# Relational graph layer: node products in chunks of four groups with the weights stationary, a ring of eight slots and 46 message buffers

## The chip, the cores and the metric

One core of a Trainium2 chip runs the kernel. Its engines are TensorE (PE; its weight loads are listed as PEld), VectorE (DVE), ScalarE (ACT), GpSimd (POOL) and SyncE (SP). The metric is the device time of one launch in microseconds, the median of several runs.

## The reference

12,500 nodes with 256 features, 212,500 edges sorted by destination (100,000 random ones in both directions and one loop edge per node), each with one of eight types. `weight` has 8 x 256 x 256, `loop_weight` 256 x 256 values; all is float32.

```python
def reference(x, src, dst, edge_type_8, weight, h_bias, loop_weight):
    h = relu((x - mean(x)) / sqrt(var(x) + 1e-05))          # per row
    hx = einsum('ni,rio->rno', h, weight)
    msg = hx[edge_type, src]
    agg = segment_sum(msg, dst, num_segments=12500)
    return x + agg * 0.5 ** 0.5 + h_bias + (h @ loop_weight) * 0.5 ** 0.5
```

## The kernel before

The kernel exchanges the two steps: it first sums, for every node and type, the h rows of the node's incoming edges, and then multiplies these sums by the weights. Edges are worked in tiles of up to 128 (1583 of them); two tiles are a unit (792 units, each of at most 271 edges' advance). Four stages run side by side, and their instructions are issued in an order that Python writes out by hand in one loop over the tiles t.

- **Gather** (`gather`, L779 to L793). POOL issues one indirect DMA for a tile: 128 rows of 1 KB of h (or of x, for the first tiles, normalized afterwards on DVE and ACT in batches of four) go to a message buffer. `MSGS` = 66 buffers stand in pairs; at tile t the gather of tile t + `AHEAD` (64) is issued, so POOL waits when PE has not yet finished the sums of the pair whose buffers it needs. A gather is a DMA of the software queue.
- **Sums** (`edge_sums`, L822). For both halves of the features PE multiplies the message rows (stationary) by a one-hot matrix (moving, L795) of 22 or 13 nodes x 8 types, that is 176 or 104 columns. A float32 product runs as two passes, each with its own weight load, so a tile has four loads and four matmuls on L837. The sums of a unit stay in one of four PSUM banks until DVE adds them to the ring (`add_sums`, L847, L851) one unit later.
- **The ring** `acc` (L288) holds, transposed, the sums of the nodes at hand: 128 features x 2 halves x 8 types x nodes. It has `SLOTS` = 6 slots of 128 nodes. A group is 128 nodes, one slot. `Plan` gives for each group the first unit that may touch its nodes (`first`) and the last one (`last`). A slot is prepared for group g + 6 when group g is done: by `clear` (ACT, zeros), or later by `begin` (L890), which lets PE transpose the group's own h rows to the tile `pt`, DVE write them, multiplied by the loop edge's type, in eight writes (L900), and ACT keep a copy `self_t` (L883). The types of the loop edges are found per four groups by `mark` and `find_types` (L913 to L967). When the ring comes round, `wrap` (L1007) adds its overhang.
- **Products** (`group_work`, L1014). For each group 18 products (loop weight and eight types, two halves of the inputs each) are accumulated in a PSUM tile `po`: the group's sums (128 features x 128 nodes) are stationary, the weights (256 columns) move. With two passes each that is 36 loads and 36 matmuls on L1029. Then `finish` adds a bias copy and the product to the rows of x (L1041, L1042), and after four groups stores 512 rows by one DMA on SP. `finish` also prepares the slot for group g + 6. `group_ahead` (L985) loads the next x and h rows.

When do products run? Once the last unit of group g is added, its 18 products enter `queue` with the earliest tile `ready` (six tiles on), the latest tile `until` (before the unit `first` of group g + 6) and a cost each; at every tile so many are taken that all are in time (L1233 to L1240). For the last eight groups (`SOON`) `until` is at most six tiles after `ready`. Jobs that need `pt` go one after the other through `shared` and `advance` (L677 to L703), DVE's writes of own rows are held back by `credit` (L1191, L1221), and `late` holds what falls due at a tile.

At the start, the gathers of the first 64 tiles are issued, and 26 pieces of x are normalized to the table h in DRAM, three in four tiles. When the last is through (`norms_end`, L1150), the weights are loaded and scaled, and gathers read h from 72 tiles on.

Of the kernel before, what the change touches and what calls it, by code (L numbers as in the profile page):

```python
# [43 lines left out]
SLOTS = 6  # L44
# [3 lines left out]
MSGS = 66  # L48
AHEAD = 64
# [170 lines left out]
def kernel(  # L220
# [63 lines left out]
    with ExitStack() as main:  # L284
# [12 lines left out]
        early = main.enter_context(tc.tile_pool(name="early", bufs=1))  # L297
        marks = main.enter_context(tc.tile_pool(name="marks", bufs=1))
        selves = main.enter_context(tc.tile_pool(name="selves", bufs=SLOTS + 1))
# [13 lines left out]
        outs = [ps_o.tile([P, 2, D], F32, name=f"po{i}") for i in range(2)]  # L313
# [533 lines left out]
        def add_sums(u, ps):  # L847
            a = acc[:, :, :, bass.ds(offsets.pop(u), WIN)]
            a = dataclasses.replace(a, dep_tracking_offset=order)
            ps = ps.rearrange("p c (d r) -> p c r d", r=R)  # L850
            i = nc.vector.tensor_tensor(a, a, ps, op=ALU.add)  # L851
            added[u] = i.ins
            for g in range(1, plan.NG):
                if plan.first[g] == u:
                    while plan.first[g] and (g, "slot") not in zeroed:
                        advance(None)
                    assert not plan.first[g] or (g, "slot") in zeroed
                    for k in [k for k in zeroed if k[0] == g or k[1] == "wrap"]:
                        tc.add_manual_dep(
                            i.ins, zeroed.pop(k).name, SYNC_DEP, reason="columns are empty")  # L860

# [8 lines left out]
        def turn_nodes(g, pool, written=None):  # L870
# [10 lines left out]
            def keep():  # L881
                got["self", g] = pool.tile([P, KC, GROUP], F32, name="self_t")
# [7 lines left out]
        def begin(g):  # L890
# [4 lines left out]
            turn, keep, pst = turn_nodes(g, selves, written)  # L895
# [89 lines left out]
        def group_ahead(g):  # L985

            q, k = divmod(g, XG)

            def load(q):
                load_groups("x", x, q)  # L990
                if q < plan.typed:
                    load_groups("h", h32, q)

            work = []
            if g == 0:
                work.append((0.0, lambda: load(0)))
            if q < plan.typed:
                def turned_nodes():
                    turn, keep, _ = turn_nodes(g, early)
                    shared(turn, [(1, keep)])  # L1000

                work.append((0.4, turned_nodes))
            if k == XG - 2:
                work.append((0.0, lambda: load(q + 1)))
            return work
# [8 lines left out]
        def group_work(g):  # L1014
# [3 lines left out]
            first_dep = [True]  # L1018

            def product(r, c):  # L1020
                if (r, c) == (R, 0):
                    got["out", g] = outs[g % 2][:, 0, :]
# [4 lines left out]
                else:  # L1027
                    lhs, rhs = acc[:, c, r, s0 : s0 + n], w[:, c, r * D : (r + 1) * D]
                i = nc.tensor.matmul(got["out", g][:n], lhs, rhs, start=(r == R and c == 0),  # L1029
                                     stop=(r == R - 1 and c == KC - 1))  # L1030
                latest["pe"] = i.ins
                if (r, c) == (R, 0) and g < 2:
                    tc.add_manual_dep(i.ins, done["bias"], SYNC_DEP, reason="one engine at a time")
                if r < R and first_dep[0]:
                    first_dep[0] = False
                    tc.add_manual_dep(i.ins, added[plan.last[g]].name, SYNC_DEP, reason="sums complete")

            def finish():
                q, k = divmod(g, XG)
                rows_ = got["x", q]  # L1040
                nc.vector.tensor_add(rows_[:n, k, :], rows_[:n, k, :], outs[g % 2][:n, 1, :])  # L1041
                nc.vector.tensor_add(rows_[:n, k, :], rows_[:n, k, :], got["out", g][:n])  # L1042
                if XG * (q + 1) >= plan.NG:
                    nc.sync.dma_start(out[d0 : d0 + n], rows_[:n, k, :])
                elif k == XG - 1:
                    first = plan.starts[XG * q]
                    nc.sync.dma_start(
                        out[first : d0 + n].rearrange("(k p) d -> p k d", p=P), rows_)
                b = g + SLOTS
                q, k = divmod(b, XG)  # L1050
                if b < plan.NG:
                    if q < plan.typed:
                        clear(b)
                    else:
                        begin(b)
                if q + 1 >= plan.typed and XG * (q + 1) < plan.NG:
                    if k == XG // 4:
                        load_groups("h", h32, q + 1)
                    if k == XG - 2:
                        mark(q + 1)  # L1060
                    if k == XG - 1:
                        find_types(q + 1)

            def last():
                done["late"].append((done["tile"] + REST, finish))

            work = []
# [6 lines left out]
        with tc.manual_schedule():  # L1074
# [56 lines left out]
            def load_weights():  # L1131
                bias_in = got["bias"] = rowp.tile([P, XG, D], F32, tag="rows", name="biasr")[:, 0, :]
                nc.sync.dma_start(
                    bias_in, bass.AP(tensor=bias.tensor, offset=bias.offset, ap=[[0, P], [1, D]]))
# [6 lines left out]
            def scale_weights():  # L1141
                for o in outs:
                    i = nc.vector.tensor_copy(o[:, 1, :], got["bias"])
                done["bias"] = i.ins.name
# [27 lines left out]
            next_group = 0  # L1172
# [13 lines left out]
            for t in range(NT):  # L1186
# [56 lines left out]
                while waiting and (len(waiting) > LAG or t == NT - 1):  # L1243
                    u, ps = waiting.pop(0)
                    add_sums(u, ps)
                    while (next_group < plan.NG and plan.last[next_group] <= u
                           and (done["weights"] or (NT <= 400 and done["norm"] == len(pieces)))):
                        g = next_group
                        while background and NT <= 400:
                            step()  # L1250
                        until = PAIR * (plan.first[g + SLOTS] - 3) - REST if g + SLOTS < plan.NG else NT - 1
                        ready = t + max(0, min(DELAY, NT - 1 - t - 2 * DELAY))
                        if g >= plan.NG - SOON:
                            ready = min(ready, t + 1)
                        until = max(ready, min(until, ready + int(GROUP / plan.rate * PAIR)))
                        if g >= plan.NG - SOON:
                            until = min(until, ready + DELAY)
# [45 lines left out]
```

## Time and profile before

| what | value |
|---|---|
| median of 3 runs | 2439.66 us (2438.91 to 2439.7) |
| the profiled execution | 2440.51 us, its span 2438.7 us |
| mean granted clock of TensorE | 0.893 |
| PE, PEld, DVE, ACT, POOL busy | 79%, 70%, 54%, 9%, 62% |
| gathers | 1483 from h, 100 from x, 207.59 MB in all |
| waits of POOL's gathers | issue 438.9 us (1324), unknown queue 219.5 us (122), PE sums L837 91.8 us (79) |
| waits of DVE's adds L851 | unknown 377.3 us, PE sums L837 272.6 us |
| DMA, mean | 114 GB/s |

Busy PE counts modelled ends of overlapping matmuls, so the distance from one start to the next says more than a duration. "issue" is time in which an engine waits for nothing that the profile shows. The profile's clock row gives tenths of full speed for 40 slices of the span.

### The profile page before, as it was taken

How to read it: one execution, taken by the hardware profiler on the slowest of the kernel's cores; microseconds unless marked ns; L12 is line 12 of the kernel's file. 1: busy time of each engine (PE TensorE's matmuls, PEld its weight loads, DVE VectorE, ACT ScalarE, POOL GpSimd, SP SyncE). 2: the span in 40 equal slices, each digit the busy share in tenths (PEclk: the TensorE clock that was granted, in tenths of full speed). 3: DMA queues.
4: the chain of work that ended last, by engine and by line, in shares of the span. 5: the costliest groups of instructions: out<-in, count | busy, mean ns of one | idle time of the engine just before them, and what ended most of it. 6: DMA issues, size and time to landing. Idle time of an engine off the chain costs nothing.

```text
span 2438.7 us, 28985 instructions
## 1 busy us (share of the span) xinstructions
PE 1934.7 (79%) x10339; PEld 1700.9 (70%) x10339; DVE 1326.8 (54%) x3382; ACT 222.2 (9%) x475; POOL 1508.5 (62%) x1609
## 2 busy tenths in 40 slices
PE   0257788787888888888888888888888888888889
PEld 0246677776777777777777777777777777777788
DVE  3387734546744545754445754445754445765453
ACT  3474310000000000000000000000000000000000
POOL 7535666666666666666666666666666666666640
PEclk9557989999989898998889998899899889998999
DMA  6584433343334343333343333343333343333320
GB/s 204 161 296 137 125 89 117 89 127 114 91 117 119 89 124 116 91 117 105 105 123 91 116 116 93 115 127 89 117 117 89 118 118 92 117 106 101 111 71 14
DMA packets 147869, 278.87 MB, mean 114 GB/s; under 512 B 29759, under 2 KB 97064, under 8 KB 147720
## 3 DMA queue, kind: packets, MB, share of 16 engines
q0 software_dynamic: 75984, 207.59, 29.2%
q1 hardware_dynamic: 70136, 69.38, 8.9%
q8 instruction: 82, 1.34, 0.2%
q14 instruction: 67, 0.55, 0.1%
q10 hardware_dynamic: 1600, 0.01, 0.0%
HBM read 251.26 MB, written 25.60 MB: 114 GB/s over the span
## 4 chain that ended last, share of the span: by engine, by line
PE 66%; issue 14%; DVE 11%; another core or an unknown queue 4%; ACT 2%; DMA 1%; POOL 1%; DVEq 0%; SPq 0%; ACTq 0%; POOLq 0%
PE ps L837 33%; PE po L1029 31%; DVE acc L851 2%; DVE oh L804 1%; DVE e_stats L741 1%; DVE acc L900 1%; PE pt L878 1%; DVE n_stats L741 1%; DVE moves L380 1%; DVE n_mv L743 1%; POOL msg L791 1%; DMA w<-in_L_gnn_weight_dram 1%; DVE fixed L382 0%; ACT diagonal L954 0%
## 5 line engine op out<-in xcount | busy, mean ns | idle before, releaser
L791 POOL DMA_INDIRECT msg<-h,gidx x1483 | 1411.6, 952 | 761.5 <-issue 389.6
L837 PE MATMUL ps<-oh,msg 128*128 128x176 f32 (+1 forms) x6332 | 1178.9, 314 | 303.2 <-issue 163.0
L837 PEld LDWEIGHTS ps<-oh,msg 128*128 128x128 f32 x6332 | 1090.1, 208 | 444.6 <-issue 217.5
L1029 PE MATMUL po<-w,acc 128*128 128x256 f32 x3136 | 975.0, 413 | 87.5 <-issue 75.5
L851 DVE TENSOR_TENSOR acc<-acc,ps 128x352 f32 x792 | 409.0, 516 | 764.4 <-remote 377.3
L1029 PEld LDWEIGHTS po<-w,acc 128*128 128x128 f32 x3136 | 577.8, 206 | 164.8 <-issue 132.2
L804 DVE TENSOR_TENSOR oh<-fixed,cols 128x704 f32<-128x704 f32 x397 | 348.9, 879 | 0.0
L900 DVE SCALAR_TENSOR_TENSOR acc<-types,pt 128x256 f32<-128x256 bf16 (+1 forms) x688 | 248.7, 411 | 89.2 <-PE ps L837 48.5
L883 ACT ACTIVATE self_t<-pt 128x256 f32<-128x256 f32 x98 | 37.5, 383 | 1754.2 <-DVE acc L900 1030.5
L791 POOL DMA_INDIRECT msg<-in_x_dram,gidx x100 | 95.0, 950 | 83.1 <-issue 49.3
L1029 PE MATMUL po<-wl,self_t 128*128 128x256 f32 x392 | 116.6, 410 | 14.3 <-issue 7.7
L1029 PEld LDWEIGHTS po<-wl,self_t 128*128 128x128 f32 x392 | 70.9, 201 | 35.5 <-issue 24.0
L878 PE MATMUL pt<-ident,hr 128*128 128x128 f32 x196 | 41.7, 288 | 29.0 <-issue 25.7
L1041 DVE TENSOR_TENSOR xr<-xr,po 128x256 f32<-128x256 f32 x98 | 40.6, 415 | 31.1 <-remote 14.5
L753 ACT ACTIVATE msg<-msg,e_shift,e_rstd 128x256 f32<-128x256 f32 x100 | 51.8, 589 | 21.3 <-DVE e_shift L750 12.0
L753 ACT ACTIVATE xt<-xt,n_shift,n_rstd 128x256 f32<-128x256 f32 x98 | 50.9, 589 | 18.5 <-DVE e_stats L741 6.1
L878 PEld LDWEIGHTS pt<-ident,hr 128*128 128x128 f32 x196 | 25.9, 156 | 30.2 <-issue 25.9
L954 ACT ACTIVATE diagonal<-ident,kinds 128x128 bf16<-128x128 f32 x88 | 28.1, 390 | 172.7 <-DVE kinds L950 158.6
L1042 DVE TENSOR_TENSOR xr<-xr,po 128x256 f32<-128x256 f32 x98 | 41.2, 421 | 3.4
L380 DVE TENSOR_SCALAR moves<-fixed 128x271 int32<-128x271 int32 (+1 forms) x90 | 40.5, 450 | 2.2 <-issue 0.9
L382 DVE COPY_PREDICATED fixed<-moves,fixed 128x311 int32<-128x311 int32 (+14 forms) x90 | 38.0, 422 | 3.1
L741 DVE BATCH_NORM_STATS2 e_stats<-msg 128x6 f32<-128x256 f32 x100 | 34.9, 410 | 0.0
(242 smaller groups left out, 354.8 us busy)
## 6 DMA issues: line engine op xcount, KB each, us to landing
msg<-h,gidx POOLq DMA_INDIRECT x1483
xt<-in_x_dram SPq DMA_DIRECT2D x24, 512.0 KB
h<-xt SPq DMA_DIRECT2D x24, 512.0 KB
xr<-in_x_dram SPq DMA_DIRECT2D x24, 512.0 KB
hr<-h SPq DMA_DIRECT2D x24, 512.0 KB
out_dram<-xr SPq DMA_DIRECT2D x24, 512.0 KB
w<-in_L_gnn_weight_dram SPq DMA_DIRECT2D x2, 1024.0 KB
msg<-in_x_dram,gidx POOLq DMA_INDIRECT x100
```

The costliest lines, as they stand in the source:

```text
L380: nc.vector.tensor_single_scalar(m, packed[:, :n], 1 << (bit + k), op=ALU.bitwise_and)
L741: nc.vector.bn_stats(stats[:n, j, :], rows_[j])
L753: nc.scalar.activation(rows_[j], rows_[j], AF.Relu, bias=shift[:n, j : j + 1], scale=rstd[:n, j : j + 1])
L791: nc.gpsimd.indirect_dma_start(out=msg[t], out_offset=None, in_=table[:, :], in_offset=bass.IndirectOffsetOnAxis(ap=gidx[b][:, at : at + 1 ...
L804: j = nc.vector.tensor_tensor(o[:, k : k + v, :i, :], iota_f.unsqueeze(1).unsqueeze(1).to_broadcast([P, v, i, C]), of.unsqueeze(3).to_broa ...
L837: j = nc.tensor.matmul(ps[:, c, :width], m[:, c * P : (c + 1) * P], o[:, :width], start=(i == 0 and c == 0), stop=(end and c == KC - 1))
L851: i = nc.vector.tensor_tensor(a, a, ps, op=ALU.add)
L878: nc.tensor.transpose(pst[:, c, :n], rows_[:n, c * P : (c + 1) * P], ident[:n, :n])
L900: i = nc.vector.scalar_tensor_tensor(acc[:, :, r, s0 : s0 + n], of, float(r + 1), pst[:, :, :n], op0=ALU.is_equal, op1=ALU.mult)
L1029: i = nc.tensor.matmul(got["out", g][:n], lhs, rhs, start=(r == R and c == 0), stop=(r == R - 1 and c == KC - 1))
L1041: nc.vector.tensor_add(rows_[:n, k, :], rows_[:n, k, :], outs[g % 2][:n, 1, :])
L1042: nc.vector.tensor_add(rows_[:n, k, :], rows_[:n, k, :], got["out", g][:n])
```

## The change

The products of four groups (a chunk) are done together, and the operands change places: a 128 x 128 block of the weights is stationary and the sums of 512 nodes move. So the result comes out transposed (outputs x nodes), in two PSUM tiles, one for each half of the outputs. ACT copies each to `flat` and adds the bias, now a column; PE turns eight blocks back by transposes; DVE adds two pairs of groups to the rows of x. A chunk has 72 passes of 512 columns where four groups had 144 of 256. The last six groups (`ALONE`) are done singly as before, with the bias as a row.

The ring has eight slots, the message buffers are 46, and 44 tiles are gathered ahead. `self_t` is kept per chunk, in two buffers. A chunk may start (`ready`) three tiles after the last sums of its fourth group, and must end (`until`) `ROOM` = 7 tiles before the first tile of the group that reuses its first slot. That slot's own rows are turned five tiles earlier and written at once when the chunk is through; the other three slots follow at intervals of `STEP` = 13 tiles. Types and h rows are loaded per chunk. `add_sums` asks for prepared slots before its add and not after it.

```diff
-SLOTS = 6
+SLOTS = 8
+CHUNK = 4
+ALONE = 6
+STEP = 13
+ROOM = 7
+EARLY = 5
...
-MSGS = 66
-AHEAD = 64
+MSGS = 46
+AHEAD = 44
...
-        selves = main.enter_context(tc.tile_pool(name="selves", bufs=SLOTS + 1))
+        selves = main.enter_context(tc.tile_pool(name="selves", bufs=2))
...
-        outs = [ps_o.tile([P, 2, D], F32, name=f"po{i}") for i in range(2)]
+        outs = [ps_o.tile([P, CHUNK * GROUP], F32, name=f"po{i}") for i in range(KC)]
+        flat = ring.tile([P, KC, CHUNK * GROUP], F32, name="flat")
+        bias_row = ring.tile([P, D], F32, name="bias_row")
+        bias_col = ring.tile([P, KC], F32, name="bias_col")
...
             def write():
+                if not free():
+                    assert done["tile"] < NT - 1
+                    active.insert(0, (done["tile"] + 1, write, False))
+                    return
                 for r in range(R):
-                    writes.append((g, 0.42, lambda r=r: own(r)))
-
-            shared(turn, [(2, write), (2, keep)], lambda: q in typed)
+                    writes.append((g, 0.0 if at_once else 0.42, lambda r=r: own(r)))
+
+            if at_once:
+                jobs.insert(0, (turn, [(2, write), (3, keep)], lambda: q in typed, done["tile"], False))
+            else:
+                shared(turn, [(2, write), (3, keep)], lambda: q in typed)
...
+        def freed(g, **how):
+
+            b = g + SLOTS
+            if b < plan.NG:
+                if b // XG < plan.typed:
+                    clear(b)
+                else:
+                    begin(b, **how)
+
+        def types_ahead(q, t):
+
+            if plan.typed <= q and XG * q < plan.NG:
+                later(t, lambda: load_groups("h", h32, q))
+                later(t + STEP, lambda: mark(q))
+                later(t + STEP + 4, lambda: find_types(q))
...
+        def chunk_work(q, until):
+
+            g0 = CHUNK * q
+            s0 = g0 % SLOTS * GROUP
+            width = CHUNK * GROUP
+            first_dep = [True]
+
+            def product(h, r, c):
+                half = slice(h * P, (h + 1) * P)
+                if r == R:
+                    while any(("self", g0 + k) not in got for k in range(CHUNK)):
+                        advance(None)
+                    lhs, rhs = wl[:, c, half], got["selves", q][:, c, :]
+                else:
+                    lhs = w[:, c, r * D + h * P : r * D + (h + 1) * P]
+                    rhs = acc[:, c, r, s0 : s0 + width]
+                multiply(outs[h], lhs, rhs, r, c, g0 + CHUNK - 1, first_dep)
+
+            def keep(h):
+                nc.scalar.activation(
+                    flat[:, h, :], outs[h], AF.Identity, bias=bias_col[:, h : h + 1], scale=1.0)
+
+            def turn_back():
+                for k in range(CHUNK):
+                    for h in range(KC):
+                        at = k % 2 * D + h * P
+                        nc.tensor.transpose(
+                            outs[k // 2][:, at : at + P], flat[:, h, k * GROUP : (k + 1) * GROUP], ident)
+
+            def finish():
+                rows_ = got["x", q]
+                for i in range(CHUNK // 2):
+                    pair = rows_[:, 2 * i : 2 * i + 2, :]
+                    nc.vector.tensor_add(pair, pair, outs[i].rearrange("p (k d) -> p k d", k=2))
+                d0 = plan.starts[g0]
+                nc.sync.dma_start(
+                    out[d0 : d0 + width].rearrange("(k p) d -> p k d", p=P), rows_)
+
+            through = []
 
             def last():
-                done["late"].append((done["tile"] + REST, finish))
-
-            work = []
-            for r in [R, *range(R)]:
-                for c in range(KC):
-                    work.append((0.55, lambda r=r, c=c: product(r, c)))
+                through.append(True)
+                t = done["tile"]
+                done["banks"] = [(t + REST, turn_back), (t + 2 * REST, finish)]
+                done["late"] += done["banks"]
+                done["late"].sort(key=lambda a: a[0])
+                first = 0 if g0 + SLOTS < XG * plan.typed else 1
+                for k in range(first, CHUNK):
+                    later(t + 1 + STEP * k, lambda k=k: freed(g0 + k))
+                types_ahead(q + 3, t + 2)
+
+            if XG * plan.typed <= g0 + SLOTS < plan.NG:
+                later(until - EARLY, lambda: freed(g0, free=lambda: bool(through), at_once=True))
+            work = [(0.0, lambda: load_both(q + 1))] if XG * (q + 1) < plan.NG else []
+            for h in range(KC):
+                for r in [R, *range(R)]:
+                    for c in range(KC):
+                        work.append((0.8, lambda h=h, r=r, c=c: product(h, r, c)))
+                work.append((0.0, lambda h=h: keep(h)))
             work.append((0.0, last))
             return work
...
+                        if len(part) > 1:
+                            ready = t + REST
+                            until = max(ready, PAIR * plan.first[g + SLOTS] - ROOM)
+                            work = chunk_work(g // CHUNK, until)
+                        else:
+                            ready = t + 1 if g >= plan.NG - SOON else t + DELAY
+                            until = ready + DELAY
+                            work = alone_work(g)
```

More of the change, by code (lines that the diff above doesn't have):

```diff
@@ L847, in add_sums @@
         def add_sums(u, ps):
+            empty = []
+            for g in range(1, plan.NG):
+                if plan.first[g] == u:
+                    while plan.first[g] and (g, "slot") not in zeroed:
+                        advance(None)
+                    empty += [zeroed.pop(k) for k in [k for k in zeroed if k[0] == g]]
             a = acc[:, :, :, bass.ds(offsets.pop(u), WIN)]
@@ L852, in add_sums @@
             added[u] = i.ins
[L853 to L860, printed above, removed]
+            for j in empty:
+                tc.add_manual_dep(i.ins, j.name, SYNC_DEP, reason="columns are empty")
         def clear(g):
@@ L1028, in product @@
                     lhs, rhs = acc[:, c, r, s0 : s0 + n], w[:, c, r * D : (r + 1) * D]
[L1029 to L1036, printed above, removed]
+                multiply(o, lhs, rhs, r, c, g, first_dep)
@@ L1171 @@
             late = done["late"]
[L1172 removed]
+            full = max(0, (plan.NG - ALONE) // CHUNK) * CHUNK
+            parts = [list(range(g, g + CHUNK)) for g in range(0, full, CHUNK)]
+            parts += [[g] for g in range(full, plan.NG)]
+            next_part = 0
             load_offsets(0)
@@ L1249 @@
                         while background and NT <= 400:
                             step()
[L1251 to L1257, printed above, removed]
+                        if not next_part:
+                            load_both(0)
```

117 lines of the change are left out of this document (57 added, 60 removed).

## The prediction

> **What bounds the kernel now.** I read the page first, then the costliest groups, then POOL's and PE's timelines over the same stretch, then windows near the end. Start with the page: engines and clock.
>
> ```profile
> span 2438.7 us, 28985 instructions
> ...
> PE 1934.7 (79%) x10339; PEld 1700.9 (70%) x10339; DVE 1326.8 (54%) x3382; ACT 222.2 (9%) x475; POOL 1508.5 (62%) x1609
> ...
> PEclk9557989999989898998889998899899889998999
> ```
>
> No engine is full and TensorE's clock is not either. The groups give the two candidates.
>
> ```profile
> L791 POOL DMA_INDIRECT msg<-h,gidx x1483 | 1411.6, 952 | 761.5 <-issue 389.6
> L837 PE MATMUL ps<-oh,msg 128*128 128x176 f32 (+1 forms) x6332 | 1178.9, 314 | 303.2 <-issue 163.0
> L1029 PE MATMUL po<-w,acc 128*128 128x256 f32 x3136 | 975.0, 413 | 87.5 <-issue 75.5
> L851 DVE TENSOR_TENSOR acc<-acc,ps 128x352 f32 x792 | 409.0, 516 | 764.4 <-remote 377.3
> ```
>
> POOL starts a gather every 0.95 + 0.30 = 1.252 us when it can (0.30 is its usual gap below), yet from tile 90 to tile 1501 the trace has 1411 tiles in 2051.8 us (270.6 to 2322.4), 1.454 us each. PE's own need is less: in undisturbed stretches a 176-column pass starts 0.148 us after the last, a 104-column one 0.112, a 256-column one 0.216. A tile has four ps passes (0.59 or 0.45, mean 0.52 us, 8 instructions counting weight loads) and 36 x 98 / 1583 = 2.23 product passes (0.48): 1.00 us and some 12.8 instructions. Neither 1.00 nor 1.252 explains 1.454. First POOL's, then PE's timeline shows what does.
>
> ```profile
> 1228.84 0.95 POOL L791 DMA_INDIRECT msg<-h,gidx  x1 [0.30 <-issue]
> 1230.10 0.95 POOL L791 DMA_INDIRECT msg<-h,gidx  x1 [0.30 <-issue]
> 1233.04 0.95 POOL L791 DMA_INDIRECT msg<-h,gidx  x1 [1.99 <-PE ps L837]
> ```
>
> ```profile
> 1227.74 1.15 PE L837 MATMUL ps<-oh,msg 128*128 128x176 f32 x4
> 1228.73 0.38 PE L1029 MATMUL po<-w,acc 128*128 128x256 f32 x1
> 1229.90 0.38 PE L1029 MATMUL po<-w,acc 128*128 128x256 f32 x1 [0.79 <-issue]
> 1230.12 0.47 PE L837 MATMUL ps<-oh,msg 128*128 128x104 f32 x3
> 1231.33 0.25 PE L837 MATMUL ps<-oh,msg 128*128 128x104 f32 x1 [0.74 <-issue]
> 1232.04 0.69 PE L1029 MATMUL po<-w,acc 128*128 128x256 f32 x2 [0.47 <-issue]
> 1232.57 0.90 PE L837 MATMUL ps<-oh,msg 128*128 128x176 f32 x4
> ```
>
> After eight gathers in a row PE, waiting for nothing, issues one load or matmul per 0.70 us or a multiple of it; POOL then reaches its limit (64 tiles ahead), pauses 1.99 us, and PE runs freely again. Between 400 and 2290 us the instruction times hold 129 such groups of slow starts (over 0.55 us apart), 411 us in all; 110 end inside a pause of POOL, 1.6 us after it begins. From a pause's end to the next slow start pass 8.0 us or 91 PE instructions in the mean. So **PE and POOL are locked**: PE pays for continuous gathering, and only a full set of buffers stops POOL. The lead stayed between 57 and 66 tiles from tile 60 to 1519. Two windows with the gathers on and off complete it (columns: busy us of PE, PEld, DVE, ACT, POOL, then clock).
>
> ```profile
> 2310.00:2350.00 40.00, 33.69 (x206) 30.08 (x205) 21.17 (x50) 2.64 (x7) 25.57 (x27) 1.00 0.38 108
> 2360.00:2400.00 40.00, 40.00 (x242) 38.03 (x241) 20.77 (x37) 0.00 (x0) 0.00 (x0) 1.00 0.00 1
> ```
>
> Without gathers PE never stumbles, though it issues faster.
>
> **A model of the lock, checked on this kernel.** PE runs free for 8.0 us and does 8.4 tiles (0.955 us for a tile with two product passes); POOL issues 6.4; the lead drops by 2.0. Then PE needs 12.8 x 0.70 = 9.0 us a tile and POOL catches up in 2.0 / (1/1.252 - 1/9.0) = 2.9 us; add a pause of 2.0: 12.9 us for 8.7 tiles, 1.48 us each. Seen: 1.454. With 91 instructions in place of 8.0 us it gives 1.53.
>
> **The change, part by part.** Times are against the profiled execution, 2440.51 us with a span of 2438.7; the median of the runs, 2439.66, differs by 0.04%, so I use the span.
>
> *Products.* 92 of 98 groups go into 23 chunks of 72 passes with 512 columns instead of 144 with 256. No row has a 512-column f32 pass. The rows at 176 and 256 rise by 0.85 ns a column: 0.43 us. Lower bound: 0.216 (were the pass all overhead); upper: 0.86, at the half clock seen below. I take 0.43, since 176 and 256 lie on one line through nearly zero. A chunk then streams 72 x 0.43 = 31.0 us against 144 x 0.216 = 31.1: **nothing gained in streaming**. Half the loads go, but a load (0.21 us, behind a 0.216 pass) was already hidden. PE's instructions fall by 92 x 72 - 23 x 144 - 368 = 2944 of some 20,700, 14%.
>
> *Turning back.* 184 transposes; a pair of them adds 0.22 us to a tile (1.25 against 1.03), so 0.11 each, 0.9 us a chunk. Twice that if cold. 46 ACT evictions of 512 columns at 0.6 us (types, L965: 0.597) fall on an engine 9% busy. DVE loses 196 adds at 0.42 (82 us), gains 46 of 512 columns at 0.5 to 0.84 and 12 of 0.42; it is idle 46% and PE does not wait for it there, so I count 0. If that cover went, it would be a gain of some 40 us. The bias as a column, and four ring wraps fewer at 0.88 us, are nothing beside this. SP issues the same 512 KB loads and stores, a little earlier or later; the x, h and out transfers land well before use, 0 again.
>
> *Where the products stand.* This is what moves. By the plan's arithmetic a chunk may start 3 tiles after its fourth group's sums, and must end 7 tiles before the first tile that may touch the reused slots: 17 to 19 tiles (21 and 25 for the last two) of the 64.1 from one chunk to the next. Before, a group's 18 products were spread over its 16 tiles. Now the window holds 18 x 0.52 + 31.0 + 0.9 = 41.3 us, 2.3 us a tile, with POOL idling half of it; I add 2 us for a half-clock start: 43.3. At 1.252 us POOL could do 34 gathers in that, but only as far as its buffers allow. The other 46.1 tiles hold sums alone. The same model there: free for 8.0 us, 15.4 tiles; POOL 6.4, lead down 9.0; PE at 8 x 0.70 = 5.6 us a tile, POOL catches up in 9.0 / (1/1.252 - 1/5.6) = 14.5 us; with the pause 24.5 us for 18.0 tiles, **1.36 us**, and 1.41 by instructions. A stretch that ends in its free part saves up to 7 us, part of which the next window pays back. I take 1.23 in the mean, 56.7 us. Period: 43.3 + 56.7 = 100.0, against 2051.8 / 22 = 93.3 now. Break-even needs 1.08 us a tile there.
>
> *Waits.* Eight own-type writes (8 x 0.41 = 3.3 us of DVE) stand behind the window's last product; the adds queue behind them, and PE has four banks (8 tiles, 4 us) before it would notice: 0, or 3 us a chunk without that cover. The chunk's first product waits for sums 3 tiles old, before 6: up to 1.6 us more, taken as 0.
>
> *Buffers 66 to 46, 44 ahead.* The lead drawn on was 7 tiles of 64, so 0 in the middle; if the cover were needed, 20 gathers or 25 us once. At the start 20 tiles fewer come from x and need normalizing (DVE 0.41 + 0.16, ACT 0.59 each); tile 40 stays at 194.5 us, and tiles 40 to 90 at 1.35 put tile 90 at 262 (was 270.6). At the end, from tile 1501: 82 tiles, 46 us; a chunk and six groups, 31 + 6 x 7.8 = 78; turning and last store 7; stumbles 7: 138 (was 116.3).
>
> **Sum:** 262 + 22 x 100.0 + 138 = 2600 us.
>
> The Trainium skill (TensorE: Matmul & The Clock Gate, Part 1) says that the array's clock drops to half after an idle window of about 3.4 us and returns after a busy one. The trace agrees in kind: 0.51 in the stretch from 1148.0 to 1154.5 us, after a stumble, then 1.00. That rule would make the sums-only stretches cold throughout, the third rival below.
>
> **Rivals.** (1) *PE draws on the 44 buffered tiles.* If sums-only stretches don't stumble, PE outruns POOL there and POOL refills during windows; POOL never pauses. Period 64.1 x 1.252 = 80.3, 262 + 22 x 80.3 + 138 = 2167 us. For it: between 2310 and 2345, where products are already bunched, 28 tiles take 35.5 us, 1.27 each, and PE's timeline has nine tiles of sums in a row there:
>
> ```profile
> 2319.05 4.93 PE L837 MATMUL ps<-oh,msg 128*128 128x176 f32 x36
> ```
>
> Against: those stretches have 8 to 10 tiles, within one free run; 46 are not. It decides as soon as they go below 1.08. (2) *Only the instruction count matters.* Stumbles fall 14% wherever the products stand: PE's surplus per period is 93.3 - 67 = 26, less 14% is 3.7, minus little else: 89.6 to 91, about 2390 us. For it: 91 instructions per free run. Against: a window cannot pass at less than 2.3 us a tile. The Trainium skill (Runtime: NRT & Kernel Launch, Instruction fetch mechanics) holds code fetch to be mostly hidden; by that this rival gains nothing, 2440 us. Code loads here (82 of 16 KB, one per 30 us) go on after 2355 us without a stumble. (3) *Sums run cold.* At half clock a tile costs 1.04, a free run has 7.7 tiles, and the model gives 1.49: period 112, 2864 us. For it: clock 0.50 from 150 to 200 us, with PE busy 23.4 of 50. Against: 1.00 through the bunched part. (4) The two effects cancel: 2440.
>
> **Chances.** Forecast 0.63, own range 2470 (period 94.1) to 2750 (106.9). Rival 1: 0.12; 2: 0.12; 3: 0.10; 4: 0.03. No change means within 0.2%, which this measurement can tell. Slower 0.63 + 0.10 = 0.73, faster 0.24, same 0.03. The range runs from 2340, taking in rival 2, to 2750; rivals 1 and 3 stay out.
>
> **What would show it.** Right: sums-only tiles at 1.1 to 1.4 us with slow starts ended by POOL pauses; windows of 18 tiles taking over 40 us with POOL pausing per pair; 512-column starts 0.43 us apart; PE instructions down 14%. Wrong: POOL without pauses outside the windows, a lead swinging by 15 or more, or DVE or SP named as what PE waits for.

## The result and the profile after

The changed kernel takes 2563.86 us (median of 6 runs, 2561.05 to 2582.0), the kernel before 2439.68 us in the same comparison: a ratio of 1.0522, with a 95% interval of 1.0501 to 1.0544. It is slower, as forecast (2600 us). The execution that was profiled is the longest of the six, 2582.0 us with a span of 2580.3; the stages below are read from it.

The page of the changed kernel, first its head, then some groups (busy time and mean ns of one, then the idle time just before them and what ended most of it):

```profile
span 2580.3 us, 26024 instructions
...
PE 1957.4 (76%) x8867; PEld 1461.0 (57%) x8867; DVE 1270.3 (49%) x3184; ACT 238.9 (9%) x496; POOL 1503.3 (58%) x1605
...
PEclk9566988988988978978889889789788788798899
...
L798 POOL DMA_INDIRECT msg<-h,gidx x1503 | 1425.6, 949 | 933.4 <-PE ps L844 367.1
L844 PE MATMUL ps<-oh,msg 128*128 128x176 f32 (+1 forms) x6332 | 1174.0, 337 | 364.0 <-issue 145.9
L864 DVE TENSOR_TENSOR acc<-acc,ps 128x352 f32 x792 | 409.1, 517 | 945.8 <-PE ps L844 556.4
L977 PE MATMUL pt<-diagonal,ones_b 128*128 128x512 bf16 x22 | 12.2, 556 | 153.1 <-ACT diagonal L970 103.8
```

PE has 14.2% fewer instructions (8867 matmuls for 10339), yet PE, PEld, DVE and POOL are busy for a smaller share, ACT stays at 9%, and the idle time before POOL's gathers from h grew from 761.5 to 933.4 us. So nothing became full; more time is lost in waits. L977, 22 instructions that spread the node types, now sees 153.1 us of idle time before it.

By the starts of the sums (L837 before, L844 after) the three parts of the span are, on the time axis of the profile (the prediction's 270.6 and 116.3 us differ from it by 0.3 us):

| part | before | after | forecast |
|---|---|---|---|
| start to tile 90 | 270.9 us | 242.9 us | 262 us |
| tiles 90 to 1501 | 2051.9 us | 2200.6 us | 2200 us |
| tile 1501 to the end | 116.0 us | 136.8 us | 138 us |

The loss is in the middle (+148.7 us) and at the end (+20.8), the start gains 28.0. In the middle a period of four groups takes 100.1 us in the mean: a window of 17.7 tiles, from the first product pass to the last, in 44.6 us (2.51 us a tile), and 46.6 tiles behind it in 55.5 us (1.19 us a tile). The expectations below count a sums-only tile from the turning back on, some three tiles later: 43.1 tiles in 52.8 us, 1.226 us a tile.

What these tiles without products wait for is best seen in one of them. First DVE's timeline, then POOL's, of the changed kernel (start, duration, engine, line, operation, tiles; in brackets the idle time before and what ended it):

```profile
626.95 0.52 DVE L864 TENSOR_TENSOR acc<-acc,ps 128x352 f32 x1 [2.05 <-PE ps L844]
636.15 0.16 DVE L956 TENSOR_SCALAR place__3858<-pt 128x4 f32<-128x4 f32 x1 [8.68 <-remote]
636.35 0.16 DVE L958 TENSOR_TENSOR place__3858<-place__3858,pt 128x4 f32<-128x4 f32 x1
```

```profile
628.72 0.95 POOL L798 DMA_INDIRECT msg<-h,gidx  x1 [0.30 <-issue]
629.97 0.95 POOL L798 DMA_INDIRECT msg<-h,gidx  x1 [0.30 <-issue]
631.22 0.94 POOL L798 DMA_INDIRECT msg<-h,gidx  x1 [0.30 <-issue]
632.47 0.95 POOL L798 DMA_INDIRECT msg<-h,gidx  x1 [0.30 <-issue]
636.40 0.94 POOL L798 DMA_INDIRECT msg<-h,gidx  x1 [2.98 <-remote]
```

And PE's:

```profile
623.31 0.35 PE L950 MATMUL pt<-loops,mark 128*128 128x24 bf16 x8 [1.17 <-issue]
623.51 2.33 PE L844 MATMUL ps<-oh,msg 128*128 128x104 f32 x16
638.98 0.58 PE L977 MATMUL pt<-diagonal,ones_b 128*128 128x512 bf16 x1 [13.14 <-ACT diagonal L970]
```

PE finished L950 at 623.7 us. DVE's L956 needs only that, and still starts at 636.15, ended by "remote", a release that the profile cannot place. All that time POOL sends one gather after the other; it stops at 633.4, when it waits for buffers, and DVE moves 2.7 us later. PE waits 13.14 us behind the chain DVE, ACT, PE. It is the prediction's disturbance, but on DVE, and PE inherits it as a wait for ACT.

The trace also records the signals (semaphore increments) with which one engine releases another, and here it is the signal that is late. PE starts no matmul between 625.53 and 638.98 us; the seven signals of the matmuls that end between 623.66 and 625.85 are recorded between 636.05 and 636.34, and DVE and POOL go on at that moment.

### The profile page after: what moved, and what is told of

It is laid out like the page before. It is cut to its first block, busy times and chain, and to the rows that moved or that the text cites. A ratio compares the mean times of both kernels' runs of the same rounds, so it can differ in the third digit from the quotient of the medians.

```text
span 2580.3 us, 26024 instructions
## 1 busy us (share of the span) xinstructions
PE 1957.4 (76%) x8867; PEld 1461.0 (57%) x8867; DVE 1270.3 (49%) x3184; ACT 238.9 (9%) x496; POOL 1503.3 (58%) x1605
## 4 chain that ended last, share of the span: by engine, by line
PE 60%; issue 13%; DVE 12%; another core or an unknown queue 9%; ACT 2%; DMA 2%; POOL 1%; DVEq 1%; SPq 0%; ACTq 0%; POOLq 0%
PE po L1049 30%; PE ps L844 28%; DVE acc L864 3%; DVE acc L909 2%; DVE oh L811 1%; DVE e_stats L748 1%; PE pt L884 1%; POOL msg L798 1%; ACT diagonal L970 1%; DMA msg<-h,gidx 1%; DVE moves L387 1%; DVE n_stats L748 1%; PE po L1115 1%; DMA h<-xt 1%
## 5 line engine op out<-in xcount | busy, mean ns | idle before, releaser
L798 POOL DMA_INDIRECT msg<-h,gidx x1503 | 1425.6, 949 | 933.4 <-PE ps L844 367.1
L844 PEld LDWEIGHTS ps<-oh,msg 128*128 128x128 f32 x6332 | 1094.2, 226 | 644.2 <-issue 395.5
L844 PE MATMUL ps<-oh,msg 128*128 128x176 f32 (+1 forms) x6332 | 1174.0, 337 | 364.0 <-issue 145.9
L864 DVE TENSOR_TENSOR acc<-acc,ps 128x352 f32 x792 | 409.1, 517 | 945.8 <-PE ps L844 556.4
L1049 PE MATMUL po<-acc,w 128*128 128x512 f32 x1472 | 721.9, 610 | 16.7 <-issue 11.6
L1049 PEld LDWEIGHTS po<-acc,w 128*128 128x128 f32 x1472 | 264.4, 195 | 212.7 <-issue 201.8
L977 PE MATMUL pt<-diagonal,ones_b 128*128 128x512 bf16 x22 | 12.2, 556 | 153.1 <-ACT diagonal L970 103.8
L798 POOL DMA_INDIRECT msg<-in_x_dram,gidx x80 | 75.9, 948 | 79.7 <-issue 35.4
L1108 ACT ACTIVATE flat<-po,bias_col 128x512 f32<-128x512 f32 x46 | 31.6, 687 | 936.3 <-PE po L1049 812.3
L1049 PE MATMUL po<-self_t,wl 128*128 128x512 f32 x184 | 95.7, 633 | 0.5 <-ACT self_t L892 0.5
L977 PEld LDWEIGHTS <-ones_b 128*128 128x128 bf16 x22 | 2.3, 106 | 128.4 <-DVE one L964 107.7
L884 PE MATMUL pt<-ident,hr 128*128 128x128 f32 x196 | 46.8, 327 | 26.2 <-issue 10.2
L970 ACT ACTIVATE diagonal<-ident,kinds 128x128 bf16<-128x128 f32 x88 | 28.1, 390 | 263.8 <-DVE kinds L966 228.6
L1049 PEld LDWEIGHTS po<-self_t,wl 128*128 128x128 f32 x184 | 35.0, 205 | 24.6 <-issue 23.2
L884 PEld LDWEIGHTS pt<-ident,hr 128*128 128x128 f32 x196 | 29.5, 171 | 34.2 <-issue 13.1
L1049 PE MATMUL po<-w,acc 128*128 128x256 f32 (+1 forms) x192 | 47.4, 387 | 0.7 <-issue 0.6
L760 ACT ACTIVATE msg<-msg,e_shift,e_rstd 128x256 f32<-128x256 f32 x80 | 41.5, 588 | 21.4 <-DVE e_shift L757 8.3
```

What stands on the lines that cost most here:

```text
L760: nc.scalar.activation(rows_[j], rows_[j], AF.Relu, bias=shift[:n, j : j + 1], scale=rstd[:n, j : j + 1])
L798: nc.gpsimd.indirect_dma_start(out=msg[t], out_offset=None, in_=table[:, :], in_offset=bass.IndirectOffsetOnAxis(ap=gidx[b][:, at : at + 1 ...
L844: j = nc.tensor.matmul(ps[:, c, :width], m[:, c * P : (c + 1) * P], o[:, :width], start=(i == 0 and c == 0), stop=(end and c == KC - 1))
L884: nc.tensor.transpose(pst[:, c, :n], rows_[:n, c * P : (c + 1) * P], ident[:n, :n])
L970: nc.scalar.activation(marked[q][:, g * GROUP : (g + 1) * GROUP], ident, AF.Copy, scale=kinds[:, g : g + 1])
L1049: i = nc.tensor.matmul(o, stationary, moving, start=(r == R and c == 0), stop=(r == R - 1 and c == KC - 1))
```

## The experiments

Each ratio is to the kernel before, run on the same chip. They met three chips, of two kinds. On two of them the kernel before takes 2440 to 2462 us; on the third, which had the first four experiments, 2023.56 us, and there the late starts are absent. Where I compare stages across runs, both profiles come from the same kind.

**On the chip without late starts.** First, weights stationary and the new ring and store, but no windows:

```diff
-CHUNK = 4
+CHUNK = 2
...
-                            until = max(ready, PAIR * plan.first[g + SLOTS] - ROOM)
+                            until = max(ready, min(ready + 28, PAIR * plan.first[min(g + SLOTS, plan.NG - 1)] - ROOM))
```

> The changed kernel with products of two groups at once instead of four: weights stationary, 256 nodes moving, results turned back, ring of eight and 46 buffers as in the change, but the 36 passes of a pair are spread evenly over about 28 tiles, as the kernel before spreads them. If putting the products into a window is what costs (a sums-only tile stays near 1.23 us because POOL's gathers hold PE back, while a window tile takes 2.2), the tiles go back to 1.45 to 1.50 us and the time to 2400 to 2480 us. If the stationary weights, the turning back or the smaller store of messages cost, it stays at 2540 to 2600 us. If the products are free once their weights are stationary, it falls below 2350 us.

Second, windows but sums stationary (72 passes of 512 become 144 of 256, nothing turned back):

```diff
-                    lhs = w[:, c, r * D + h * P : r * D + (h + 1) * P]
-                    rhs = acc[:, c, r, s0 : s0 + width]
-                multiply(outs[h], lhs, rhs, r, c, g0 + CHUNK - 1, first_dep)
+                    s = s0 + k * GROUP
+                    lhs, rhs = acc[:, c, r, s : s + GROUP], w[:, c, r * D : (r + 1) * D]
+                at = k % 2 * D
+                multiply(outs[k // 2][:, at : at + D], lhs, rhs, r, c, g0 + CHUNK - 1, first_dep)
```

> The other half: the changed kernel's windows, ring and buffers, but the products as in the kernel before, sums stationary and 256 columns of weights moving, 144 passes a chunk of four groups instead of 72 of 512; nothing is turned back, the bias is added on VectorE. If the window is what costs, the time stays with the changed kernel, 2540 to 2640 us. If the stationary weights cost, it goes to 2400 to 2460 us. If the number of PE instructions counts (1.45/91 PE instructions a tile of the lock in the prediction), it is 64 to 130 us above the changed kernel, 2630 to 2700 us.

Third, the types' spreading later:

```diff
-            shared(spread, [(1, types_of)], lambda: q in marked, wait=2 * SETTLE)
+            shared(spread, [(1, types_of)], lambda: q in marked, wait=6 * SETTLE)
```

> The changed kernel, the spreading of the node types (the product of ones and diagonal) queued 24 tiles after the types are found instead of 8, so that ScalarE has the diagonal ready. If PE's waits for ScalarE and VectorE in that chain (153 us of idle time before the 22 spreads) are what sets the sums-only stretches, the time falls by 100 to 150 us, to 2410 to 2470 us. If POOL's gathers set them, PE loses the time elsewhere: 2535 to 2570 us, 0 to 30 us gained, and the sums-only tile stays at 1.20 to 1.25 us.

Fourth, the kernel before with half the bytes of its 1483 gathers from h (it leaves out the second half of each row, and its sums use the first half twice):

```diff
-                out=msg[t], out_offset=None, in_=table[:, :],
+                out=msg[t][:, :P] if kind[t] == "h" else msg[t], out_offset=None,
+                in_=h32.rearrange("n (a c) -> (n a) c", a=KC) if kind[t] == "h" else x[:, :],
```

> The kernel before, the 1,503 gathers from h fetching 128 columns of a row (512 bytes) instead of 256, the first half of the message buffer used for both halves of the sums; PE, VectorE and POOL issue the same instructions, the output is not the reference's. If the number of gathers that POOL issues sets the pace of PE (a gather 1.25 us, the lock), the time stays at 2400 to 2450 us. If it is the bytes or their landing (DMA traffic, the late message), it falls toward PE's own need of 1.0 to 1.1 us a tile, 1850 to 2100 us.

| run | us | ratio | 95% interval |
|---|---|---|---|
| pairs_spread | 2049.26 | 1.0121 | 1.0104 to 1.0138 |
| bunched_sums | 2075.3 | 1.0253 | 1.0236 to 1.0270 |
| types_late | 2078.47 | 1.0268 | 1.0251 to 1.0285 |
| half_rows | 2021.73 | 0.9987 | 0.9977 to 0.9996 |

The times cannot be held against what was expected, because the chip is another (half_rows falls into a range given for the bytes for that reason alone). Read against each other they say more. From 400 to 1900 us, busy us and instructions of PE, PEld, DVE, ACT and POOL, then clock, DMA share and GB/s. First the changed kernel on the chip of the prediction:

```profile
400.00:1900.00 1500.00, 1173.46 (x5359) 861.47 (x5358) 746.47 (x1736) 70.67 (x167) 916.48 (x966) 0.86 0.35 102
```

Then types_late, the changed kernel but for that one wait, on the other chip:

```profile
400.00:1900.00 1500.00, 1357.94 (x6672) 979.68 (x6672) 924.19 (x2176) 88.14 (x207) 1136.88 (x1193) 0.96 0.43 126
```

POOL issues 1193 gathers here, 1500 / 1193 = 1.257 us each: it is the bound, at the pace of 1.252 us that it has when nothing holds it. A tile without products takes 0.82 us in the mean, and single tiles 0.62. The mean period is 79.6 us; rival 1 of the prediction had worked out 80.3. From 400 to 1900 us the lead there swings between 3 and 21 tiles, against 35 to 46 in the changed kernel on the other chip. In that stretch no wait of DVE over 1 us in sum ends with "remote" there, against 203 us for its adds L864 in the changed kernel on the other chip. So nothing in the program forces 1.226 us. bunched_sums has the same windows with passes of 256 columns and is as slow as types_late, so the width of the passes does not matter on this chip. That half the bytes change nothing (0.13%) says that on this chip the number of gathers counts, not their size; with late starts it was not tried.

What the change costs there stands in POOL's pauses. Its last gather starts at 1997.7 us in half_rows and at 2042.1 in types_late; of these 44 us, 38 are longer pauses in the first 400 us (50 in all, against 12). pairs_spread has 35 us of pauses there too, so the store of 46 and the ring at the start are the likely reason, argued and not shown.

**Where the starts are late, a first set.** The changed kernel again; the kernel before with the small store (`MSGS` 46, `AHEAD` 44); and the kernel before with rests for POOL:

```diff
+            if t % 8 == 7:
+                for _ in range(5):
+                    nc.gpsimd.iota(
+                        pause, pattern=[[1, 256]], base=0, channel_multiplier=0)
```

> The changed kernel, unaltered, a second time. The four runs so far met a chip on which PE's slow starts are not there and the kernel before takes 2024 us, with POOL issuing gathers nearly without a pause; the changed kernel's own time on such a chip is not known. If PE's slow starts while POOL issues gathers are what made the change dear, and POOL's 1583 gathers of 1.252 us bound both kernels where they are absent, it takes 2070 to 2085 us there, a ratio of 1.02 to 1.03, and spreading the types late gained nothing. If the slow starts play no part in the change's cost, the ratio stays at 1.05, 2125 us. Where the slow starts are back, it takes 2560 us.

> The kernel before with the change's store of messages alone: 46 buffers and gathers 44 tiles ahead instead of 66 and 64. Where POOL bounds the kernel, its pauses in the first 400 us (12 us before, 50 us with the changed kernel's store) should come with the store: 2050 to 2065 us against 2024. If the pauses come from the windows, it stays at 2020 to 2030 us. Where the slow starts are back, the theory that POOL waits for buffers anyhow says 0 to 20 us more than 2440.

> The kernel before, with five small fills on POOL (some 0.35 us each) after every eighth gather, so that POOL never issues more than 10 us of gathers without a rest of about 1.7 us. Where POOL bounds the kernel, a tile goes to 1.252 + 1.7/8 = 1.47 us and the time to 2300 to 2380 us. Where the slow starts are back, the theory that back-to-back gathers bring them says that they go and the time falls from 2440 to 2320 to 2400 us; if they have another cause, it stays at 2440 us or rises.

| run | us | ratio | 95% interval |
|---|---|---|---|
| after_again | 2584.61 | 1.0488 | 1.0471 to 1.0506 |
| before_46 | 2446.73 | 0.9930 | 0.9914 to 0.9947 |
| paced | 2429.98 | 0.9866 | 0.9849 to 0.9882 |

The kernel before takes 2462.34 us here. The loss is reproduced. The small store alone costs nothing, it gains 0.7%, which I had not expected: tile 40 starts at 172.0 us, as in the changed kernel (173.8). And **paced** is the clearest of all: POOL is given 985 more instructions, and the kernel is faster, though by 32 us where I expected 40 at the least. The reason can be read in DVE's first microseconds. The kernel before (its first profile), without rests:

```profile
22.56 0.18 DVE L743 BATCH_NORM_AGGREGATE n_mv<-n_stats 128x2 f32<-128x6 f32 x1 [0.53 <-DVE n_mv L743]
23.95 0.18 DVE L743 BATCH_NORM_AGGREGATE n_mv<-n_stats 128x2 f32<-128x6 f32 x1 [1.21 <-DVE n_mv L743]
25.35 0.18 DVE L743 BATCH_NORM_AGGREGATE n_mv<-n_stats 128x2 f32<-128x6 f32 x1 [1.22 <-DVE n_mv L743]
25.45 0.14 DVE L749 RECIPROCAL n_rstd<-n_rstd 128x4 f32<-128x4 f32 x1
29.55 0.16 DVE L750 SCALAR_TENSOR_TENSOR n_shift<-n_mv,n_rstd 128x4 f32<-128x4 f32 x1 [3.96 <-remote]
```

paced, the same steps:

```profile
22.62 0.36 DVE L744 BATCH_NORM_AGGREGATE e_mv<-e_stats 128x2 f32<-128x6 f32 x4
22.90 0.14 DVE L750 RECIPROCAL n_rstd<-n_rstd 128x4 f32<-128x4 f32 x1
23.08 0.16 DVE L751 SCALAR_TENSOR_TENSOR n_shift<-n_mv,n_rstd 128x4 f32<-128x4 f32 x1
```

Four of L743 take 0.36 us when DVE can start them; without rests, after some fifteen gathers in a row, they start 1.4 us apart. The sums begin at 27.0 us in paced and at 60.5 in the kernel before. From tile 90 on paced gains nothing (2075 us to tile 1501; 2052 in the profile of the kernel before, which is from another chip of this kind), and its last 82 tiles take 143 us for 116: POOL with its rests is slower, 1.47 us a tile, and PE now waits for messages:

```profile
PEld ps L842 <- DMA msg<-h,gidx: 524.5, 517, 6.0
...
PE ps L842 <- DMA msg<-h,gidx: 341.0, 256, 5.6
```

The Trainium skill (SBUF — State Buffer, Who interferes with whom) says that in the access to SBUF only VectorE and GpSimd can block each other, through a shared port pair, and that TensorE and ScalarE wait on nobody. In the kernel before PE too starts one instruction per 0.70 us, and ACT's L745 stands idle 5.66 us before 28.86 us, ended by "remote"; so that pair cannot be the whole cause, and the rule does not cover what is seen.

**Where the starts are late, a second set**: the two open questions again, and short rests (two small fills after every third gather) in the changed kernel and in the one before.

```diff
+            if t % 3 == 2:
+                for _ in range(2):
+                    nc.gpsimd.iota(
+                        pause, pattern=[[1, 64]], base=0, channel_multiplier=0)
```

> The kernel with weights stationary for two groups at once and products spread evenly over 28 tiles, a second time, for a chip on which PE's slow starts are there (the kernel before 2440 to 2462 us, the changed one 2564 to 2585). If it is the windows that cost there, the time is near the kernel before, ratio 0.99 to 1.02, 2440 to 2490 us; if it is the stationary weights with the turning back, it is near the changed kernel, ratio 1.04 to 1.06. On a chip without slow starts the ratio is 1.012 again.

> The changed kernel with the spreading of the types 24 tiles later, a second time, for a chip with the slow starts. If PE's waits for ScalarE and VectorE in the types' chain set the sums-only stretches there, the ratio falls from 1.049 to between 0.99 and 1.01. If PE's slow starts set them, the time goes elsewhere: ratio 1.035 to 1.05, a sums-only tile 1.18 to 1.24 us. On a chip without slow starts the ratio is 1.027 again.

> The changed kernel with two small fills on POOL (together some 0.5 us) after every third gather, so that POOL is slower by 0.16 us a gather, 1.41 us. If POOL's back-to-back gathers hold PE at 1.23 us a sums-only tile, this tile falls to 0.8 to 1.1 us and the time from 2575 to 2300 to 2480 us although POOL does more; if the waits on VectorE and ScalarE or the windows alone set it, the time stays at 2560 to 2620 us. On a chip without slow starts POOL bounds the kernel: 1583 x 1.41 + 60 = 2290 us.

> The kernel before with the same two small fills after every third gather instead of five larger ones after every eighth: 1.41 us a gather instead of 1.52. If any short rest keeps PE from its slow starts, POOL bounds the kernel and the time is 1583 x 1.41 + 30 = 2260 us, below both kernels (ratio 0.92 to 0.95). If the rests have to make up a share of the time (they are 11% here, 20% with five fills after eight), some slow starts are back and it takes 2300 to 2430 us. If the rests have nothing to do with it, 2440 us or more. On a chip without slow starts it is 2260 us too, slower than the kernel before.

| run | us | ratio | 95% interval |
|---|---|---|---|
| pairs_again | 2455.68 | 1.0058 | 1.0036 to 1.0080 |
| types_again | 2588.7 | 1.0593 | 1.0569 to 1.0617 |
| after_paced | 2501.19 | 1.0233 | 1.0205 to 1.0262 |
| paced_light | 2444.36 | 1.0013 | 1.0003 to 1.0022 |

The kernel before takes 2440.63 us. pairs_again settles most of which part of the change costs: with the same operands, the same turning back, ring and store, spreading the products leaves 0.6% of the 5%. It is **the windows**. (Its passes have 256 columns again, twice as many; but a pass of 512 takes 0.430 us in the median, twice the 0.216 of 256, so the width itself costs nothing that is seen.) types_again was to clear the types' chain. PE's wait for L970 is gone, and the time is not; the lines of the changed kernel's L884 and then of types_again:

```profile
L884 PE MATMUL pt<-ident,hr 128*128 128x128 f32 x196 | 46.8, 327 | 26.2 <-issue 10.2 <-DVE gidx L372 6.6 <-DVE offs L656 3.9
```

```profile
L844 PE MATMUL ps<-oh,msg 128*128 128x176 f32 (+1 forms) x6332 | 1174.7, 338 | 440.6 <-DVE acc L864 174.3 <-issue 170.3 <-ACT msg L760 67.1
...
L884 PE MATMUL pt<-ident,hr 128*128 128x128 f32 x196 | 47.0, 329 | 106.1 <-DVE one L964 68.6 <-issue 18.1 <-DVE place__6547 L958 9.4
...
L977 PE MATMUL pt<-diagonal,ones_b 128*128 128x512 bf16 x22 | 9.5, 430 | 9.5 <-issue 6.0 <-ACT self_t L892 3.3
```

L977's idle time fell from 153.1 to 9.5 us. Half came back before the sums L844 (440.6 for 364.0), the other half before L884 (106.1 for 26.2), which turns own rows and waits for DVE's L964, an earlier step of the same chain. A sums-only tile takes 1.25 us, above the 1.18 to 1.24 expected, and the ratio too lies above its range. So ACT's step was not the cause but the place where the wait showed; the chain itself is not cleared, since PE still waits for DVE's late steps in it. after_paced slows POOL by rests of some 11% and gains about half of what the change lost: a sums-only tile falls from 1.226 to 1.157 us, the period from 100.1 to 97.3. Both are just outside the expected ranges on the weak side. paced_light misses: the same rests bring the kernel before nothing, neither the 2260 us of one theory nor the 2300 to 2430 of the other, and its slow starts stay (between 400 and 1900 us, 243 starts of PE 0.65 to 0.8 us after the last, against 270 in the kernel before and 39 in paced). Rests have to be long, or a large share; which of the two is open.

**A version that beats both.** The rests of paced, for the first 136 gathers only:

```diff
-            if t % 8 == 7:
+            if t % 8 == 7 and t < 136:
```

> The kernel before, with the five fills on POOL after every eighth gather, but for the first 136 gathers only. With fills throughout, tile 90 began at 209 us instead of 271, while tiles 90 to 1501 took 2075 us instead of 2052. If the fills pay at the start alone, this version takes 2440 - 60 = 2370 to 2395 us where the slow starts are (ratio 0.970 to 0.982), below both kernels; if what they bring at the start is lost again later, 2425 to 2445 us. On a chip without slow starts the start loses 15 to 25 us: 2035 to 2050 us against 2024.

It takes 2401.73 us against 2441.19, a ratio of 0.9836 (0.9822 to 0.9850). Tile 90 starts at 209.6 us as in paced, 61 us earlier than in the kernel before; 21 of them go again by tile 1501 (2072.5 us for the middle, 2051.9 before), so the time lies between the two expectations, nearer to the first. It is for chips of this kind: on the other, half_rows starts tile 0 at 27.0 us without rests; there it was not tried.

## Why the prediction was right

**The direction and the main term.** The prediction put the loss into the period: 43.3 us of window and 56.7 us of sums alone, 100.0 in all. The period is 100.1 us. The window has 17.7 tiles for 18 and takes 44.6 us, 2.51 a tile; the other 46.6 tiles take 55.5 us, 1.19 a tile for 1.23. So the two terms are each off by little more than 1 us, in opposite directions. The 512-column passes start **0.43 us** apart in the median, as taken; halving the passes gains nothing. pairs_again confirms what the sum implied, that stationary weights and turning back are near nothing.

**The lock, as a cause.** "PE and POOL are locked: PE pays for continuous gathering" seems to hold more widely than it was put. Three things speak for it together: on the chip without late starts the same sums-only tiles take 0.82 us; rests for POOL shorten them where the starts are late (1.157); and the kernel before gets faster when POOL does more at the start. It would also say why windows cost, though no run shows this step alone. Within them PE is full for 2.51 us a tile and POOL pauses, its buffers full; outside them PE could go at 0.62 us a tile, drains the store, and POOL answers with gathers in a row, under which the other engines hardly get on. Spread products let neither get so far from the other.

**Where the picture was wrong: the step on waits.** The model let PE itself issue one instruction per 0.70 us, and the step "Waits" took the adds and the chains behind the window as 0. Between 400 and 1900 us PE's starts 0.65 to 0.8 us after the last fall from 270 (189 us) to 78 (55 us); gaps of over 1.2 us rise from 51 (89 us) to 105 (307 us). These are mostly waits for DVE's adds and for the types, late because DVE and ACT start late. pairs_again shows the same shift (81 short starts in 57 us, 65 gaps over 1.2 us with 242 us) without the loss, so the shift is not the price by itself; all gaps over 0.55 us together are, with 327 us in the kernel before, 320 in pairs_again and 418 in the changed kernel. One sign that I had listed as wrong thus came true (DVE named as what PE waits for); the other two did not (POOL does pause, the lead swings by 11, not 15). That a value near 1.23 came out is in part luck: the arithmetic of PE instructions, which does not describe these waits, gave 1.36 to 1.41, and the value taken was already a discount. Rival 2, by which fewer instructions make the kernel faster, falls with the result. So does rival 3 (sums cold throughout, 2864 us): the granted clock is 0.86 from 400 to 1900 us.

**Start and end.** The step that kept tile 40 at 194.5 us failed: it starts at 173.8, and at 172.0 with the small store alone. The first sums are not earlier for it (61.9 us in before_46, 60.5 in the kernel before); the gain lies between tile 0 and tile 40, where 20 tiles fewer are normalized, and its cause stays open. That is 19 of the 20 us by which the forecast misses the profiled execution; from the median, 2563.86 us, it is off by 36. The end, 136.8 us for 138, was right.

**Rival 1** (POOL never pauses, period 80.3, 2167 us) is what the other chip does. The ground against it was the late starts, and it holds just where these are. I gave no case for a chip without them, since the one trace could not show that there is such a chip.

## What to carry to other kernels

Work that is spread evenly between two engines that disturb each other can be worth more than fewer, larger instructions: here the passes halved, and the price came from where they stood. Before a limit is laid to the program, look whether an instruction with all its inputs ready starts late, on every engine, whether the signal that releases it is late, and what else is running then; rests for the suspected engine are a cheap test. And when a wait is moved away and comes back elsewhere, look further up its chain.

## What the runs showed of the hardware

- Two kinds of chip run the same program with the same instruction durations (a gather 0.95 us, an add 0.52) in 2024 or 2440 to 2462 us. On the second, after eight to fifteen gathers in a row, PE, DVE and ACT start single instructions 0.70 to 1.4 us apart, or one not for 8.7 us, until POOL has paused for 1.4 to 2.7 us. The granted clock is lower there (0.893 for the kernel before, 0.957 in half_rows), with PE idle more. What is shared between POOL's gathers and the other engines' starts is open.
- The data are not later on that kind: a packet of the gathers takes 159 ns in the median in types_late and in the changed kernel alike, and, with 48 packets a gather taken in order, the last ends 2.42 us after the issue in both. The signals are: in types_late 99% of PE's signals between 400 and 1900 us are recorded within 0.02 us of the matmul's end. Of the gathers' signals, 16 for each of 1583 gathers, the traces from the fast chip hold 25,283 to 25,304 of 25,328, those from the other two chips 6046 to 8629. So "remote" is also what a wait shows whose release was not recorded. It suggests a rival that no run here tests: that the recording of the execution itself holds signals and engines up. Every execution on record has a span and a granted clock from the profiler, so there is no time without it.
- On that kind four kernels that spread their products and differ in rests and store need 1.46 to 1.47 us a tile from tile 90 to 1501 (before_46, paced, paced_light and pairs_again; the kernel before 1.454): 1.25 us a gather is not sustained. A fixed share would explain it; no run here tests it, and paced reaches it by its own rests.
